# A transformer kernel with routed experts: the last list of a layer in tiles of 128 rows instead of 256, and the experts' weights laid side by side in memory

## The chip, the cores and the metric

The kernel runs on one core of one Trainium2 chip. Its engines work side by side: TensorE (PE in the profile; its weight loads are PEld), VectorE (DVE), ScalarE (ACT), GpSimd (POOL) and SyncE (SP). SP computes nothing here; it reads numbers from memory and issues transfers (DMAs), in the order of its queue. All engines run their own instructions in order and wait for each other by semaphores. The metric is the time of one execution on the device in microseconds (us). A profile is one execution of it, taken by the hardware profiler.

## The reference

All data are float32. The input x has 16 sequences of 256 positions with 128 channels, which is 4096 tokens. Four steps follow each other, each added to x:

```
x = x + attention_a(layernorm(x))    # 16 heads of 8, blocks of 64 positions
x = x + ffn(layernorm(x))            # routed experts, layer 0 of the kernel
x = x + attention_b(layernorm(x))    # 16 heads of 8, over the 16 sequences at one position
x = x + ffn(layernorm(x))            # routed experts again, layer 1 of the kernel
```

The experts' step takes two of eight experts for each token:

```
logits = flat_x @ Wr                           # 4096 x 8
top_vals, top_idx = top_k(logits, 2)
rw = softmax(top_vals)                         # weights of the two experts
g = flat_x @ Wg[e];  u = flat_x @ Wu[e]        # 128 -> 512, for each expert e
h = silu(g) * u
eo = (h @ Wd[e]) / sqrt(12)                    # 512 -> 128
out = sum over the two experts of rw * eo
```

The reference computes all eight experts for each token and uses two; the kernel computes only the two, which is 8192 rows of work in each layer.

## The kernel before

**Tokens and rows.** The tokens are worked on in four quarters (q = 0 to 3) of 1024 tokens each. `router` (L590) normalizes the tokens of a quarter, chooses two experts for each and writes two rows for each token into `sorted_in` in HBM (L699): 128 channels, the weight and the place where the result belongs. Each expert has its own region there, and its rows stand in it in the order in which the quarters arrive. These writes are 16 indirect transfers a quarter, issued by POOL.

**Tiles and lists.** The experts are computed in tiles of TT = 256 rows of one expert. Which expert and which rows a tile has is known only at run time, so it is read from a table. There are three lists of tiles in a layer: the first is made when two quarters are routed (9 tiles), the second after the third (8 tiles), and the last after the fourth (22 tiles), 39 in all. The first two lists hold only full tiles. The last holds all that is left, and since each expert's rest need not fill its tile, it has room for up to seven tiles more than the rows would need. A tile that would reach past its expert's rows is moved back, and rows that were done already, or that are none, are written to places that nobody reads (`behind`). `tile_tables` (L715) computes a list on DVE.

**One tile.** `experts` (L857) runs the tiles of a layer one after another. `fetch` reads the table's row and expert into registers of SP and issues four transfers: the rows `xin` (L866), and from the three weight inputs the expert's `Wg` (L883), `Wu` (L884) and `Wd` (L885) into one tile `w`. It is called two tiles ahead; the buffers of `xin` and `w` are three each. `turned` (L891) transposes `xin` on PE (`xt`, L895), and ACT copies the result to SBUF (`xT`, L897). The hidden size of 512 is cut into four pieces of 128. A tile has two units, each with two of the four pieces: PE computes `g` and `u` for these (L953), each matmul with 256 columns, ACT the tanh (L958), DVE the rest of silu (L959) and the product `h` (L961). One unit later `down` (L900) adds `Wd` times `h` into `acc` (L903), and after a tile's second unit ACT copies `acc` to `yT` (L911), PE transposes it (`y`, L914), ACT scales it into `yo` (L919), and POOL writes the rows to `results` by their places (L926), one indirect transfer for each 128 rows. PSUM holds three buffers for `g` and `u`, one for `acc`.

**Adding the results.** `combine` (L975) reads the two results of each token back (`back`, L979), as soon as enough tiles are done that the quarter's rows must be among them (READY), and adds them to x on DVE (L989). In layer 1 it writes the output (L992). Its transfers stand in SP's queue between those of `fetch`.

**Order.** The order in which the parts are recorded is written out by hand (L1003 to the end): the generators `attention_a`, `attention_b`, `router` and `experts` are advanced step by step, and `weave` lets some run beside others. `units(layer, upto)` advances the experts to a unit. From the counts above it follows for each layer: units 1 to 30 run beside other parts, units 31 to 52 alone behind the last router (BEGIN[0] = 52); in layer 0, units 53 to 60 run beside the first normalization of attention b (FIRST = 60), and the rest to 79 beside that attention by written goals (GOAL = 62, 64, 66, 70, 74, 79); in layer 1 the rest runs alone, with `combine` between, from unit 52 to 66 and to 79. A scheduler then orders the recorded instructions on each engine, and the program is fixed before it runs.

## Time and profile before

| What | us |
|---|---|
| median of 14 runs | 976.18 |
| lowest and highest of them | 971.29, 985.98 |
| the profiled execution | 977.54 |
| its span, first to last instruction | 975.8 |
| PE busy, DVE busy in the span | 860.1, 619.3 |
| ACT busy, POOL busy | 402.8, 359.8 |

The mean granted clock of PE in the profiled execution is 0.938 of full speed. A line of a group or of the timeline names the engine, the kernel's line (L903), the operation, the tile written and the tiles read (`acc<-h,w`), and how many instructions it stands for. One fp32 matmul of the program is two matmul records. The ends of matmuls are modelled, and they are pipelined, so that the starts of two groups, one after the other, tell more than the length of one. In square brackets stands how long the engine was idle before, and what released it. In 107.69 MB and 104922 packets the DMA engines moved 110 GB/s on average.

### The profile page before, as it was taken

To read this page: it belongs to the slowest core of one execution; us is meant where nothing else is said; L and a number is where in the kernel's file an instruction comes from. 1 tells how busy PE (TensorE), PEld (TensorE's weight loads), DVE (VectorE), ACT (ScalarE), POOL (GpSimd) and SP (SyncE) were. 2 spreads that over 40 slices of the span, in tenths; PEclk is the share of its full clock that TensorE was granted. 3 is DMA by queue.
4 is the path that set the end of the run, shared out by engine and by line. 5 is a ranking of instruction groups with operands and counts; after the bars stand their busy time and mean duration, and the time that the engine had idled before them with its cause. 6 is when DMAs were issued, how large, how long until landed. Compare 5 with 4: busy or idle time off the path is not lost.

```text
span 975.8 us, 17640 instructions
## 1 busy us (share of the span) xinstructions
PE 860.1 (88%) x5992; PEld 709.7 (73%) x5992; DVE 619.3 (63%) x1749; ACT 402.8 (41%) x821; POOL 359.8 (37%) x404
## 2 busy tenths in 40 slices
PE   5987888889899999989987859957999999998893
PEld 3666666668788888877866748845777887886782
DVE  4568547657857775467867648835687784556542
ACT  3444334343434444436553435422554433343331
POOL 2112622442363474333121542251407465333322
PEclk9999879789999999999998969978999999999997
DMA  7100100041142476674120402124404466678762
GB/s 187 31 1 1 38 9 1 23 137 45 52 119 93 148 225 193 189 244 130 45 88 1 113 19 88 53 80 130 131 2 124 140 204 187 183 208 266 221 185 81
DMA packets 104922, 107.69 MB, mean 110 GB/s; under 512 B 10688, under 2 KB 80320, under 8 KB 104832
## 3 DMA queue, kind: packets, MB, share of 16 engines
q1 hardware_dynamic: 95024, 87.36, 31.0%
q0 software_dynamic: 9088, 18.89, 5.5%
q8 instruction: 48, 0.79, 0.4%
q10 hardware_dynamic: 720, 0.30, 0.1%
q14 instruction: 42, 0.34, 0.1%
HBM read 83.38 MB, written 23.13 MB: 109 GB/s over the span
## 4 chain that ended last, share of the span: by engine, by line
PE 70%; DVE 10%; DMA 8%; ACT 4%; issue 3%; POOL 3%; SPq 1%; ACTq 0%; POOLq 0%; DVEq 0%
PE g L953 12%; PE u L953 12%; PE acc L903 11%; PE o_A L446 6%; PE sc_A L416 5%; PE t_A L435 3%; DMA back<-results 2%; PE o_B L559 2%; PE v_B L359 2%; PE sc_B L522 2%; DMA results<-yo,to 2%; DMA xin<-sorted_in 2%; PE v_A L359 2%; POOL sorted_in L699 2%; ACT q_A L333 2%
## 5 line engine op out<-in xcount | busy, mean ns | idle before, releaser
L926 POOL DMA_INDIRECT results<-yo,to x156 | 153.9, 986 | 261.5 <-ACT yo L919 229.7
L903 PE MATMUL acc<-h,w 128*128 128x256 f32 x624 | 168.5, 389 | 5.9 <-DVE h L961 5.8
L953 PE MATMUL g<-xT,w 128*128 128x256 f32 x624 | 167.8, 388 | 0.7 <-ACT xT L897 0.5
L953 PE MATMUL u<-xT,w 128*128 128x256 f32 x624 | 165.3, 384 | 3.2 <-DVE th L959 3.2
L699 POOL DMA_INDIRECT sorted_in<-rows,pos_i_F x128 | 125.2, 978 | 89.0 <-DVE pos_i_F L692 34.5
L958 ACT ACTIVATE th<-g 128x512 f32<-128x512 f32 x156 | 93.4, 598 | 148.0 <-PE g L953 147.1
L959 DVE SCALAR_TENSOR_TENSOR th<-th,g 128x512 f32<-128x512 f32 x156 | 106.3, 682 | 74.6 <-ACT th L958 73.0
L903 PEld LDWEIGHTS acc<-h,w 128*128 128x128 f32 x624 | 117.9, 194 | 26.0 <-DVE h L961 9.3
L953 PEld LDWEIGHTS g<-xT,w 128*128 128x128 f32 x624 | 117.7, 195 | 18.1 <-issue 1.8
L953 PEld LDWEIGHTS u<-xT,w 128*128 128x128 f32 x624 | 112.4, 192 | 17.8 <-DVE th L959 4.7
L961 DVE TENSOR_TENSOR h<-th,u 128x512 f32<-128x512 f32 x156 | 106.6, 683 | 13.6 <-PE u L953 3.4
L416 PE MATMUL sc_A<-k_A,q_A 128*128 128x256 f32 x256 | 80.4, 424 | 20.6 <-DVE ex_A L425 13.3
L446 PEld LDWEIGHTS o_A<-va,eT_A 128*64 128x64 f32 x1024 | 62.3, 143 | 16.6 <-issue 7.9
L446 PE MATMUL o_A<-va,eT_A 128*64 128x18 f32 x1024 | 67.0, 216 | 1.4 <-ACT q_A L333 0.8
L416 PEld LDWEIGHTS sc_A<-k_A,q_A 128*128 128x128 f32 x256 | 45.9, 207 | 30.6 <-DVE ex_A L425 12.5
L424 DVE TENSOR_REDUCE mx_A<-sc_A 128x8 f32<-128x512 f32 x64 | 43.3, 682 | 36.7 <-PE sc_A L416 36.3
L911 ACT COPY yT<-acc 128x256 f32<-128x256 f32 x78 | 29.1, 372 | 87.9 <-PE acc L903 87.6
L919 ACT ACTIVATE yo<-y,xin 128x128 f32<-128x128 f32 x156 | 48.5, 366 | 30.7 <-PE y L914 30.6
L429 ACT ACTIVATE ex_A<-ex_A 128x512 f32<-128x512 f32 x64 | 40.1, 634 | 47.2 <-DVE ex_A L425 46.9
L439 ACT COPY eT_A<-t_A 128x512 f32<-128x512 f32 x64 | 36.2, 587 | 55.3 <-PE t_A L435 55.2
L454 POOL TENSOR_TENSOR xq<-xq,att_A 128x128 f32<-128x128 f32 x32 | 14.7, 458 | 116.1 <-DVE att_A L378 103.4
L359 PE MATMUL v_B<-wi_sb,xt_B 128*128 128x128 f32 x256 | 36.0, 292 | 24.1 <-DVE att_B L378 23.2
(173 smaller groups left out, 1294.5 us busy)
## 6 DMA issues: line engine op xcount, KB each, us to landing
w<-in_wg SPq DMA_DIRECT2D x78, 256.0 KB, 2.9
w<-in_wu SPq DMA_DIRECT2D x78, 256.0 KB
w<-in_wd SPq DMA_DIRECT2D x78, 256.0 KB, 4.0
xin<-sorted_in SPq DMA_DIRECT2D x78, 132.0 KB
back<-results SPq DMA_DIRECT2D x16, 512.0 KB, 5.7
results<-yo,to POOLq DMA_INDIRECT x156, 3.5
sorted_in<-zero SPq DMA_DIRECT2D x2, 1056.0 KB
sorted_in<-rows,pos_i_F POOLq DMA_INDIRECT x128, 2.4
```

The lines of the kernel that those rows point to most:

```text
L359: nc.tensor.matmul(pv[:, a * P : (a + 1) * P], lhsT=src[:, g * n + a].rearrange("p r k -> p (r k)"), rhs=w, start=True, stop=True,)
L416: nc.tensor.matmul(sc[:, v * 4 * BS : (v + 1) * 4 * BS], lhsT=qT[:, blk, 2 * v : 2 * v + 2, :].rearrange("p r k -> p (r k)"), rhs=kx[:, :, ...
L424: nc.vector.tensor_reduce(mx[:, 0:8], sc3, AX.X, ALU.max)
L446: nc.tensor.matmul(po[b * BS : (b + 1) * BS, i * 18 : (i + 1) * 18], lhsT=eT[:, b, 2 * v + i % 2, u * BS : (u + 1) * BS], rhs=vt[:, b, 2 * ...
L699: put_row = nc.gpsimd.indirect_dma_start(out=sorted_in[layer], out_offset=bass.IndirectOffsetOnAxis(ap=pos_i[:, k, g : g + 1], axis=0), in ...
L903: nc.tensor.matmul(acc[:, 0:TT], lhsT=w[:, 2, hc * P : (hc + 1) * P], rhs=h[:, j * TT : (j + 1) * TT], start=(hc == 0), stop=(hc == NHC - 1),)
L919: nc.scalar.activation(y[:, b, :], py[:, b * P : (b + 1) * P], AF.Identity, scale=t[:, b, C : C + 1],)
L926: put_row = nc.gpsimd.indirect_dma_start(out=results[layer], out_offset=bass.IndirectOffsetOnAxis(ap=to[:, b : b + 1], axis=0), in_=y[:, b ...
L953: nc.tensor.matmul(p[:, j * TT : (j + 1) * TT], lhsT=w[:, k, hs], rhs=xT, start=True, stop=True,)
L958: nc.scalar.activation(th, pg, AF.Tanh, scale=0.5)
L959: nc.vector.scalar_tensor_tensor(th, th, 1.0, pg, ALU.add, ALU.mult)
L961: beat[0] = nc.vector.tensor_tensor(h, th, pu, ALU.mult).ins
```

## The change

The last list of each layer is made of tiles of TS = 128 rows; the first two lists keep tiles of 256. The bound on the tiles in the last list goes from 22 of 256 rows to 37 of 128, as the room lost at the end of each expert's rows is at most 127 rows instead of 255. A small tile has one unit in place of two: its unit has all four pieces of the hidden size, so that `g`, `u`, the tanh and `h` keep their 512 columns, made of four matmuls of 128 columns in place of two of 256. The units of a layer go from 78 to 71. `fetch` is called up to three tiles ahead in the last list (AHEAD = 3), with five buffers for `xin` and `w`.

All eight experts' `Wg`, `Wu` and `Wd` are copied once, at the start, from the inputs into `w_all` in HBM, where each expert's three parts stand side by side in 128 rows of 1536 numbers. `fetch` then issues one transfer for the weights of a tile. One buffer of `rows` serves the router in place of two. The counts that the order goes by follow: READY counts tiles of 128 rows, BEGIN is now 52, 52, 59, 72, and GOAL 59, 59, 59, 63, 67, 72; FIRST stays 60.

```diff
+TS = P
...
+UNITS = (TOP * NTOK + (NE - 1) * TS) // TS
 LISTS = [full(LISTED)] + [full(n) - full(n - 1) for n in range(LISTED + 1, NQ)]
-LISTS.append(ALL - sum(LISTS))
+LISTS.append(UNITS - sum(LISTS) * (TT // TS))
+SIZES = [TT] * (len(LISTS) - 1) + [TS]
 KMAX = max(LISTS)
+LARGE = sum(LISTS[:-1]) * (TT // TS)
...
-READY = [sum(LISTS[:-1]) + NE - 1] * LISTED
-READY += [(TOP * n * TQ + NE * (TT - 1)) // TT for n in range(LISTED + 1, NQ + 1)]
-NJ = NTOK // TT
+READY = [LARGE + (NE - 1) * (TT // TS)] * LISTED
+READY += [(TOP * n * TQ + NE * (TS - 1)) // TS for n in range(LISTED + 1, NQ + 1)]
+AHEAD = 3
+NJ = NTOK // TS
...
+    p_in = ctx.enter_context(tc.tile_pool(name="p_in", bufs=2 + AHEAD))
...
-    rows = [const.tile([P, NG, TOP, RW], F32, name=f"rows{i}") for i in range(2)]
-    for t in rows:
-        nc.gpsimd.memset(t[:, :, :, C + 1 : RW], 0.0)
+    row = const.tile([P, NG, TOP, RW], F32, name="rows")
+    nc.gpsimd.memset(row[:, :, :, C + 1 : RW], 0.0)
...
+    w_all = dram.tile([NE, P, 3 * HID], F32, name="w_all")
...
+    for i, src in enumerate((wg, wu)):
+        late.append(
+            nc.sync.dma_start(out=w_all[:, :, i * HID : (i + 1) * HID], in_=src)
+        )
+    for n in range(NHC):
+        late.append(
+            nc.sync.dma_start(
+                out=w_all[:, :, 2 * HID + n * C : 2 * HID + (n + 1) * C],
+                in_=wd[:, n * P : (n + 1) * P, :],
+            )
+        )
...
     def experts(layer):
         def fetch(li, i):
             n = f"{layer}_{li}_{i}"
-            t = p3.tile([P, 2, RW], F32, tag="xin", name=f"xin_{n}")
+            size = SIZES[li]
+            t = p_in.tile([P, TT // P, RW], F32, tag="xin", name=f"xin_{n}")
...
             got = nc.sync.dma_start(
-                out=t.rearrange("p b r -> p (b r)"),
-                in_=sorted_in[layer][bass.ds(row, TT)].rearrange("(p b) r -> p (b r)", b=2),
+                out=t[:, 0 : size // P].rearrange("p b r -> p (b r)"),
+                in_=sorted_in[layer][bass.ds(row, size)].rearrange("(p b) r -> p (b r)", p=P),
             )
...
-            w = p3.tile([P, 3, HID], F32, tag="w", name=f"w_{n}")
-            nc.sync.dma_start(out=w[:, 0], in_=wg[bass.ds(e, 1)].rearrange("e c h -> (e c) h"))
-            nc.sync.dma_start(out=w[:, 1], in_=wu[bass.ds(e, 1)].rearrange("e c h -> (e c) h"))
+            w = p_in.tile([P, 3, HID], F32, tag="w", name=f"w_{n}")
             nc.sync.dma_start(
-                out=w[:, 2].rearrange("p (n c) -> p n c", c=C),
-                in_=wd[bass.ds(e, 1)].rearrange("e (n p) c -> p (e n) c", p=P),
-            )
+                out=w.rearrange("p i h -> p (i h)"),
+                in_=w_all[bass.ds(e, 1)].rearrange("e p h -> (e p) h"),
+            )
...
-            nc.scalar.copy(xT, pt[:, 0:TT])
+            nc.scalar.copy(xT[:, 0:size], pt[:, 0:size])
...
-        def down(li, i, t, w, elsewhere, acc, pair, h):
-            for j in range(2):
-                hc = 2 * pair + j
+        def down(li, i, t, w, elsewhere, acc, hcs, h):
+            size = SIZES[li]
+            for j, hc in enumerate(hcs):
                 nc.tensor.matmul(
-                    acc[:, 0:TT], lhsT=w[:, 2, hc * P : (hc + 1) * P],
-                    rhs=h[:, j * TT : (j + 1) * TT],
+                    acc[:, 0:size], lhsT=w[:, 2, hc * P : (hc + 1) * P],
+                    rhs=h[:, j * size : (j + 1) * size],
                     start=(hc == 0), stop=(hc == NHC - 1),
                 )
-            if pair == 1:
+            if hcs[-1] == NHC - 1:
...
-                for b in range(2):
+                for b in bs:
                     put_row = nc.gpsimd.indirect_dma_start(
...
         for at, (li, i) in enumerate(todo):
+            size = SIZES[li]
+            n = CH // size
...
-            for pair in range(2):
+            for part in range(NHC // n):
+                hcs = range(n * part, n * part + n)
...
                 for k, p in ((0, pg), (1, pu)):
-                    for j in range(2):
-                        hs = slice((2 * pair + j) * P, (2 * pair + j + 1) * P)
+                    for j, hc in enumerate(hcs):
                         nc.tensor.matmul(
-                            p[:, j * TT : (j + 1) * TT], lhsT=w[:, k, hs], rhs=xT,
+                            p[:, j * size : (j + 1) * size],
+                            lhsT=w[:, k, hc * P : (hc + 1) * P], rhs=xT[:, 0:size],
                             start=True, stop=True,
                         )
...
-                if pair == 0 and at + 2 < len(todo):
-                    fetched.append(fetch(*todo[at + 2]))
-                if pair == 0 and at + 1 < len(todo):
+                wanted = at + 2 if size == TT else min(begun + 1, at + AHEAD)
+                while begun < len(todo) and part == 0 and begun <= wanted:
+                    fetched.append(fetch(*todo[begun]))
+                    begun += 1
+                if part == 0 and at + 1 < len(todo):
                     xT_next = turned(*todo[at + 1], fetched[0][0])
...
-        known = puts[layer][: 2 * READY[q]]
+        known = puts[layer][: READY[q]]
...
-    EARLY = 2 * sum(LISTS[:-1]) - 4
+    EARLY = LARGE - 4
...
-    UNITS = 2 * ALL + 1
+    STEPPED = UNITS + 1
 
-    BEGIN = [min(2 * n + 1 + LEAD, UNITS) for n in READY]
+    BEGIN = [min(n + 1 + LEAD, STEPPED) for n in READY]
```

In `tile_tables` the sizes 256 become the list's own size; for the last list the tables have 37 columns for 22, and counts in steps of 128 rows, of which there are 32 in place of 16.

## The prediction, made before the changed kernel was run

> **What bounds the kernel now.** I read the busy shares, then stages of the span, then the order of time inside one stage, last the one place where the experts' chain runs bare.
>
> ```profile
> PE 860.1 (88%) x5992; PEld 709.7 (73%) x5992; DVE 619.3 (63%) x1749; ACT 402.8 (41%) x821; POOL 359.8 (37%) x404
> ```
>
> TensorE (PE) leads, but over the whole span. The stages (columns: stretch, its length, busy us of PE, PEld, DVE, ACT, POOL with counts, granted clock, DMA share, GB/s):
>
> ```profile
> 324.00:431.00 107.00, 104.31 (x531) 91.43 (x530) 64.78 (x158) 43.49 (x112) 52.52 (x55) 1.00 0.67 199
> 456.00:518.00 62.00, 59.26 (x577) 49.33 (x576) 47.78 (x110) 34.74 (x59) 9.48 (x9) 0.97 0.23 69
> 518.00:598.00 80.00, 60.54 (x557) 50.04 (x557) 49.06 (x151) 33.13 (x59) 29.55 (x30) 0.83 0.18 54
> 598.00:681.00 83.00, 64.80 (x592) 53.26 (x592) 51.19 (x172) 29.02 (x59) 29.29 (x31) 0.92 0.29 90
> 681.00:762.00 81.00, 76.30 (x655) 62.56 (x655) 61.49 (x192) 40.49 (x77) 35.17 (x35) 0.98 0.30 89
> 825.00:958.00 133.00, 126.94 (x613) 108.56 (x611) 70.29 (x121) 52.03 (x131) 41.81 (x43) 0.99 0.67 200
> ```
>
> Two stretches are the experts' tiles alone: 324 to 431 (end of layer 0's list, before its attention) and 825 to 958 (the whole last list of layer 1, 44 units of half a tile, counted back from the last tanh). There PE is busy 95 to 97% and bounds. In the second attention PE is busy 261 of 306 us: waits decide too. Order of time inside the first kind (start, length, engine, line):
>
> ```profile
> 801.53 0.38 PE L914 MATMUL y<-k_sb,yT 128*128 128x128 f32 x2
> 801.75 0.38 PE L895 MATMUL xt<-k_sb,xin 128*128 128x128 f32 x2
> 801.96 1.03 PE L953 MATMUL u<-xT,w 128*128 128x256 f32 x4
> 802.83 1.03 PE L903 MATMUL acc<-h,w 128*128 128x256 f32 x4
> ...
> 807.15 0.38 PE L914 MATMUL y<-k_sb,yT 128*128 128x128 f32 x2
> ```
>
> One tile is 807.15 - 801.53 = 5.62 us, a unit 2.81 us. Four 256-column records go out in 802.83 - 801.96 = 0.87 us (0.217 each); the last one's result is there 0.16 us after the next may start. Each matmul of the program is two such records. A `g` (0.87 us) stands between `acc` and `y`: the copy `yT` hides under it.
>
> For 128 columns the attention shows the rate: eight records in 599.49 - 598.60 = 0.89 us, 0.111 each.
>
> ```profile
> 598.60 1.05 PE L359 MATMUL v_B<-wi_sb,xt_B 128*128 128x128 f32 x8
> 599.49 0.39 PE L522 MATMUL sc_B<-k_B,q_B 128*128 128x128 f32 x2
> ```
>
> The last tile of the run has nothing beside it, so each hop of its chain is bare:
>
> ```profile
> 957.37 0.69 DVE L961 TENSOR_TENSOR h<-th,u 128x512 f32<-128x512 f32 x1
> 958.11 1.13 PE L903 MATMUL acc<-h,w 128*128 128x256 f32 x4 [0.26 <-DVE h L961]
> 959.34 0.37 ACT L911 COPY yT<-acc 128x256 f32<-128x256 f32 x1 [2.27 <-PE acc L903]
> 959.76 0.44 PE L914 MATMUL y<-k_sb,yT 128*128 128x128 f32 x2 [0.52 <-ACT yT L911]
> 960.24 0.63 ACT L919 ACTIVATE yo<-y,xin 128x128 f32<-128x128 f32 x2 [0.53 <-PE y L914]
> ```
>
> A hop from engine to engine costs 0.03 to 0.10 us, and a PE group that has waited takes 0.10 us more (1.13 against 1.03), as its weight load is no longer hidden.
>
> ```profile
> L911 ACT COPY yT<-acc 128x256 f32<-128x256 f32 x78 | 29.1, 372 | 87.9 <-PE acc L903 87.6
> L439 ACT COPY eT_A<-t_A 128x512 f32<-128x512 f32 x64 | 36.2, 587 | 55.3 <-PE t_A L435 55.2
> ```
>
> **Part 1, PE work.** The last list goes from 22 tiles (44 units) to 37 tiles, one unit each. A small unit is 24 records x 0.111 + 2 transposes x 0.108 = 2.88 us of PE, against 2.81. If PE stayed the bound, a layer's last list would go from 22 x 5.62 = 123.6 to 37 x 2.88 = 106.6 us, 17 less. By the Trainium skill's "Perfetto Trace Analysis", Matmuls, larger matmuls are more efficient than smaller ones; the rows above price that at 2.88 to 2.81, 2.5%, so the rule alone would not turn the sign.
>
> **Part 2, the chain of a small unit: a new wait.** In the built program of the changed kernel, PE's instructions in the last list stand in this order: rest of `acc`(k-1), `y`(k-1), `xt`(k+1), first part of `acc`(k), `g`(k+1), `u`(k+1), rest of `acc`(k), `y`(k) and so on, with 1 and 3 of the four `acc` matmuls before `g` in turns. No `g` stands between `acc` and `y` any more, and `xt`(k+1) has only one `acc` part before the `g` that needs it. ACT's order is tanh(k), `yT`(k-1), `yo`(k-1), `xT`(k+1). Everything on PE queues behind the waiting `y`, and `xT` queues behind `yo`. From the moment `u`(k) is issued (0):
> - `h`(k): `g`(k) was issued at -0.89, result -0.73, tanh (0.60) from -0.69 to -0.09, L959 (0.69) to 0.63, L961 (0.69, 0.10 later) 0.73 to 1.42; `acc`(k) may start at 1.47.
> - One `acc`(k-1) left: issued 0.22, result 0.39, `yT` from 0.49. A 128-column copy is not in the trace; from 372 ns at 256 and 587 at 512 I get 265 (ends: 213, ACT's shortest row, and 372): 0.75. `y` 0.80, result 1.13 (0.44 for two, less 0.11), `yo` (0.31, half of 0.63) 1.17 to 1.48, `xT` 1.52 to 1.79, `g` from 1.84. Meanwhile `acc`(k) one matmul 1.47 to 1.79. `g` and `u` 1.78 + 0.10 exposed load: the next unit's zero is 3.72.
> - Three left: all of the `y` to `xT` path is 0.44 later, `g` from 2.28 (`acc`(k), three matmuls, 1.57 to 2.23), next zero 4.16.
>
> Mean 3.94 us a unit, PE busy 2.88 of it. I take 3.94; the ends are 2.88 (all waits filled) and 4.6 (the sum with the copy at 372 ns and two more hops of 0.1 on each side, rounded up).
> - Layer 0, alone: units 35 to 52 are 18 before and after (both lists reach unit 34 with the large tiles and run alone to unit 52): 18 x (3.94 - 2.81) = +20.3.
> - Layer 1, 825 to 958: 133 us = 44 x 2.81 = 123.6 and 9.4 of stalls, mostly `xin` transfers behind combine's loads on SP's queue. After: 37 x 3.94 = 145.8. Stalls: between 0 and 9.4; fetches now run three tiles ahead and two transfers (not four) stand in SP's queue per tile, so transfer waits fall, but combine's twelve DVE additions of 0.6 to 0.7 us among these tiles now fall into a chain that DVE is part of. I take 4: 149.8, +16.8.
> - Layer 0, units 53 to 60 beside the first normalization of the second attention: same count, half hidden by its work; 0 to 8 x 1.13 = 9; I take +3.
>
> **Part 3, seven units fewer beside the second attention.** Units 61 to 79 (19) become 61 to 72 (12), and the written goals now put none beside the attention's first three halves (2 each before). PE work taken away: 7 x 2.88 = 20. In 518 to 598 PE idles 19 of 80 us and the clock is 0.83, so work taken from there shortens little, and where units covered waits the waits become bare. Between -20 and 0 (a loss if the clock falls further); I take -10.
>
> **Part 4, transfers.** Per tile one transfer of 768 KB and one of 66 in place of four. SP issues in 0.33 us each and idles most of the time: 0. PE's waits from 825 to 960 name `xin`, never `w`. The Trainium skill's "Perfetto Trace Analysis", DMA Optimizations, says that batching transfers under 2 KB into 4 to 8 KB can improve throughput dramatically; a weight row here goes from 0.5 and 2 KB to 6 KB. By the rows (DMA busy 0.67, no wait on `w`) the gain is 0; the rule would matter if DMA became the bound. Traffic per small tile: 786 + 68 + 66 KB in 3.94 us = 233 GB/s, over the 200 of the stretch at 0.67; 200 / 0.67 = 298 would be full. Hidden; without that cover (rate 200) a tile takes 4.6 us, +36 over 55 tiles.
> The copy of all weights (six transfers, 6.3 MB each way, behind the loads and fills on SP's queue): at the 191 GB/s of the first 25 us it takes 33 to 66 us, ending before 90; the first fetch issues at about 207, and DMA is nearly idle from 50 to 200. Cost 0, at most 2 for the loads that share its engines. Without that cover 66.
>
> **Part 5, the rest.** The last list's tables: eight DVE operations grow from 506 to 851 elements (0.67 to about 1.06) and two from 384 to 768 (0.55 to about 0.95): +3.9 us per layer. In layer 1 the table is ready at 798.6, while the fetch that reads it issues at 817.9 behind the last rows' scatter on POOL (to 814.8): cover 19 us, cost 0; without it 3.9 a layer. One `rows` buffer for two: the next router comes some 80 us later (`y_B` at 516, 596, 760), scatter long done: 0. One put instead of two at the end (1.27 us) and shorter last pieces: -1.5. Combine's loads before the second attention held an `xin` back by 3.0 us of PE idle near 430; with units of 3.94 the puts waited for are older: -2.
>
> **Sum** against the profiled execution, 977.54 us (span 975.8 and 1.7 around it): 20.3 + 16.8 + 3 - 10 - 1.5 - 2 = +26.6, 1004.1. That execution is 1.4 above the median of the 14 runs (976.18), so 1003 for a median.
>
> **Rivals.**
> 1. PE stays the bound (waits filled, unit 2.88): 18 x 0.07 = +1.3; 106.6 + 4 - 133 = -22.4; -10 - 1.5 - 2: -34.6, 942. This is the faster end. For it: PE is 95% busy in these stages today. Against it: in the new order nothing that is ready can pass the waiting `y`. It decides below the unit time at which the sum is zero: 55 units x p + 4 - 50.6 - 133 + 3 - 10 - 3.5 = 0, p = 3.46 us.
> 2. DMA becomes the bound: 4.6 us a tile if it moves no more than 200 GB/s, 1039. Against it: 24 us slices of the page at 266 GB/s.
> 3. The clock falls. After 1.24 and 0.45 us of PE idle near 820, the next 3.4 us ran at half speed:
>
> ```profile
> 820.00 0.44 PE L895 MATMUL xt<-k_sb,xin 128*128 128x128 f32 x2 [1.24 <-DMA xin<-sorted_in]
> 821.30:824.70 3.40, 3.40 (x10) 2.69 (x9) 1.61 (x3) 0.00 (x0) 0.96 (x1) 0.50 0.84 251
> ```
>
> A small unit idles 1.06 of 3.94 us, about 0.9 in such a window, half of what stood there; so I expect no fall. If every fourth of the 63 windows in 55 x 3.94 us fell, at 1.7 us each: +27, 1030. The Trainium skill's "TensorE: Matmul & The Clock Gate", Part 1, lets the clock fall after a whole idle window of about 3.4 us; the row above fell after half of one. By the rule this rival costs 0, by the row it stays possible.
> 4. Seven units fewer save all their PE work (-20, not -10): 993.
> 5. Not what it says: excluded for the counts (37 tiles of 128 rows stand in the built program).
>
> **How the numbers follow.** Chances: the chain as summed 0.55 (own range 988 to 1020), with case 4 0.14, cases 2 and 3 together 0.13, unit times under the limit of case 1 0.15, near it 0.03. The range leaves out most of case 1 and the far ends of 2 and 3, which is 2 in 10: 972 to 1030. No change means within 0.3%, about what this kernel's runs can tell apart (3 us): faster 0.15, same 0.04, slower 0.81.
>
> **What would show it.** In the stretch of the last lists: `y` rows on PE with idle "<-ACT yT" of 0.3 to 0.6 us each and `g` rows with "<-ACT xT" or `acc` rows with "<-DVE h"; th rows of ACT (one a unit) 3.9 us apart, PE busy about 75%, clock 1.00, DMA share about 0.75. PE's total falls (some 2 x 17 us) while the span grows. Wrong if th rows are under 3.5 us apart, if `xt` idles "<-DMA" every tile (case 2), or if the clock of these stretches is under 0.95 (case 3). Part 3 is wrong if the second attention, from the first `v_B` to the last `y_B` (307 us), does not get 5 to 15 us shorter.

## The result, and the profile after

The changed kernel takes 1033.59 us (median of 10 runs, 1028.35 to 1037.55), the kernel before 976.18; the ratio is 1.059, 95% interval 1.056 to 1.062. The prediction said 1003 and 972 to 1030: the sign is right, the size is half. The profiled execution has a span of 1032.9 us against 975.8, +57.1, at the same granted clock (0.939 and 0.938). One thing about the runs below has to be known: they fell on chips of two speeds, on which the kernel before took 973 to 976 or 1040 to 1050, so each ratio is to the kernel before on the same chip, and the text says "the slower chip" where it was that one.

The first line of the page (busy us of each engine, share of the span, instructions):

```profile
PE 862.3 (83%) x6684; PEld 722.4 (70%) x6684; DVE 607.4 (59%) x1751; ACT 401.6 (39%) x853; POOL 347.7 (34%) x389
```

PE's share falls from 88 to 83%, but its busy time does not fall. The stages that answer to those of the prediction (stretch, length, busy us of PE, PEld, DVE, ACT, POOL with counts, clock, DMA share, GB/s): layer 0's units 35 to 52 alone, the four quarters of the second attention, and the last list of layer 1 from unit 35.

```profile
377.00:450.00 73.00, 60.99 (x469) 54.91 (x470) 28.45 (x58) 25.43 (x74) 18.30 (x19) 0.99 0.76 243
486.00:541.00 55.00, 44.59 (x493) 36.25 (x493) 38.04 (x94) 27.11 (x42) 5.40 (x5) 0.91 0.07 23
541.00:619.00 78.00, 56.88 (x543) 47.15 (x543) 43.39 (x144) 28.81 (x50) 26.29 (x27) 0.80 0.14 41
619.00:692.00 73.00, 64.26 (x663) 57.82 (x663) 47.74 (x155) 29.69 (x66) 27.73 (x29) 0.91 0.42 131
692.00:792.00 100.00, 84.38 (x701) 69.32 (x700) 69.00 (x211) 42.66 (x81) 35.41 (x36) 0.97 0.29 89
858.00:1014.60 156.60, 127.12 (x944) 114.01 (x943) 61.20 (x121) 50.81 (x146) 36.16 (x37) 0.96 0.71 234
```

In the first and the last PE is busy 84 and 81% where it had been 95 to 97: these stretches are bound by something else now. The same 18 units took 50.6 us before, with PE busy throughout. Counted from the start of one tanh to that of another ("units 35 to 52" ends at the tanh of unit 53, "units 53 to 60" at that of unit 60), the difference is made up so:

| Stretch | before | after | difference | predicted |
|---|---|---|---|---|
| start to unit 35 of layer 0 | 374.5 | 376.9 | +2.4 | 0 |
| units 35 to 52 | 50.6 | 72.9 | +22.3 | +20.3 |
| units 53 to 60 | 28.7 | 34.1 | +5.4 | +3 - 2 |
| to the first v_B | 3.0 | 1.7 | -1.3 | 0 |
| second attention | 304.0 | 306.1 | +2.1 | -10 |
| to unit 35 of layer 1 | 64.7 | 66.5 | +1.8 | 0 |
| rest of the last list | 130.5 | 156.4 | +25.9 | +16.8 |
| after the last tanh | 19.8 | 18.3 | -1.5 | -1.5 |
| sum | 975.8 | 1032.9 | +57.1 | +26.6 |

Inside the first stretch, PE, ACT and DVE in order of time (start, length, engine, line; in brackets the idle time before and what ended it):

```profile
400.51 1.06 PE L976 MATMUL u<-xT,w 128*128 128x128 f32 x8
401.34 0.69 DVE L983 SCALAR_TENSOR_TENSOR th<-th,g 128x512 f32<-128x512 f32 x1 [2.14 <-ACT th L982]
401.41 0.83 PE L917 MATMUL acc<-h,w 128*128 128x128 f32 x6
402.33 0.27 ACT L925 COPY yT<-acc 128x128 f32<-128x128 f32 x1 [1.02 <-PE acc L917]
402.65 0.33 PE L929 MATMUL y<-k_sb,yT 128*128 128x128 f32 x1 [0.41 <-ACT yT L925]
402.81 0.16 DVE L939 TENSOR_TENSOR to<-xin,behind 128x1 int32<-128x1 f32 x1 [0.78 <-DMA xin<-sorted_in]
402.81 0.27 PE L909 MATMUL xt<-k_sb,xin 128*128 128x128 f32 x1
402.92 0.69 DVE L985 TENSOR_TENSOR h<-th,u 128x512 f32<-128x512 f32 x1
403.01 0.37 ACT L934 ACTIVATE yo<-y,xin 128x128 f32<-128x128 f32 x1 [0.42 <-PE y L929]
403.28 0.26 ACT L911 COPY xT<-xt 128x128 f32<-128x128 f32 x1
403.66 0.94 PE L917 MATMUL acc<-h,w 128*128 128x128 f32 x6 [0.57 <-DVE h L985]
404.43 1.06 PE L976 MATMUL g<-xT,w 128*128 128x128 f32 x8
```

This is the order that the prediction gave: PE stands 0.41 us before `y`, whose copy `yT` nothing hides, `xt` queues behind it, `xT` behind `yo`. One thing is there that it did not give: `to` (L939) stands on DVE between the two halves of silu and waits 0.78 us for the rows of a later tile; `h` and the `acc` behind it are late by that. The waits of PE in the whole run say the same (us in total, times, longest); before, `y` had hardly waited for `yT` (0.5 us) and `acc` 5.8 us for `h`:

```profile
PE y L929 <- ACT yT L925: 25.0, 60, 0.7
PE acc L917 <- DVE h L985: 22.5, 39, 2.0
PE ot_B L515 <- DVE att_B L393: 9.4, 3, 7.8
```

The last tile, bare as before, and the copies by their shape (busy, mean ns, idle before):

```profile
1016.69 1.16 PE L917 MATMUL acc<-h,w 128*128 128x128 f32 x8 [0.34 <-DVE h L985]
1018.26 0.33 PE L929 MATMUL y<-k_sb,yT 128*128 128x128 f32 x1 [0.41 <-ACT yT L925]
1018.62 0.37 ACT L934 ACTIVATE yo<-y,xin 128x128 f32<-128x128 f32 x1 [0.42 <-PE y L929]
...
L934 ACT ACTIVATE yo<-y,xin 128x128 f32<-128x128 f32 x142 | 48.4, 367 | 44.4 <-PE y L929 43.1 <-DMA results<-yo,to 0.8 <-DMA back<-results 0.4
L925 ACT COPY yT<-acc 128x128 f32<-128x128 f32 x74 | 19.8, 267 | 68.6 <-PE acc L917 68.6
```

The copy takes 267 ns (estimated: 265), `yo` 367 (taken: 310).

### The profile page after: what moved, and what is told of

The parts are those of the page before. It is cut to its first block, busy times and chain, and to the rows that moved or that the text cites. A ratio compares the mean times of both kernels' runs of the same rounds, so it can differ in the third digit from the quotient of the medians.

```text
span 1032.9 us, 18843 instructions
## 1 busy us (share of the span) xinstructions
PE 862.3 (83%) x6684; PEld 722.4 (70%) x6684; DVE 607.4 (59%) x1751; ACT 401.6 (39%) x853; POOL 347.7 (34%) x389
## 5 line engine op out<-in xcount | busy, mean ns | idle before, releaser
L943 POOL DMA_INDIRECT results<-yo,to x142 | 141.1, 994 | 302.0 <-ACT xT L911 148.5
L917 PE MATMUL acc<-h,w 128*128 128x128 f32 (+1 forms) x864 | 169.0, 320 | 22.9 <-DVE h L985 22.5
L983 DVE SCALAR_TENSOR_TENSOR th<-th,g 128x512 f32<-128x512 f32 x142 | 96.8, 682 | 154.3 <-ACT th L982 153.8
L976 PE MATMUL g<-xT,w 128*128 128x128 f32 (+1 forms) x864 | 159.1, 319 | 7.3 <-ACT xT L911 3.9
L976 PE MATMUL u<-xT,w 128*128 128x128 f32 (+1 forms) x864 | 155.3, 316 | 6.1 <-DVE th L983 6.1
L917 PEld LDWEIGHTS acc<-h,w 128*128 128x128 f32 x864 | 130.0, 196 | 42.9 <-DVE h L985 33.5
L976 PEld LDWEIGHTS u<-xT,w 128*128 128x128 f32 x864 | 125.4, 198 | 13.5 <-DVE th L983 8.4
L925 ACT COPY yT<-acc 128x128 f32<-128x128 f32 (+1 forms) x108 | 32.4, 300 | 116.9 <-PE acc L917 116.9
L929 PE MATMUL y<-k_sb,yT 128*128 128x128 f32 x142 | 37.5, 303 | 29.9 <-ACT yT L925 25.0
L929 PEld LDWEIGHTS y<-k_sb,yT 128*128 128x128 f32 x142 | 19.5, 141 | 48.2 <-ACT yT L925 37.8
```

The lines of the kernel that those rows point to most:

```text
L917: nc.tensor.matmul(acc[:, 0:size], lhsT=w[:, 2, hc * P : (hc + 1) * P], rhs=h[:, j * size : (j + 1) * size], start=(hc == 0), stop=(hc == ...
L929: nc.tensor.transpose(py[:, b * P : (b + 1) * P], yT[:, b * P : (b + 1) * P], ident)
L943: put_row = nc.gpsimd.indirect_dma_start(out=results[layer], out_offset=bass.IndirectOffsetOnAxis(ap=to[:, b : b + 1], axis=0), in_=y[:, b ...
L976: nc.tensor.matmul(p[:, j * size : (j + 1) * size], lhsT=w[:, k, hc * P : (hc + 1) * P], rhs=xT[:, 0:size], start=True, stop=True,)
L983: nc.vector.scalar_tensor_tensor(th, th, 1.0, pg, ALU.add, ALU.mult)
```

## Experiments on the chain of a small unit

Theory A: the order on PE and the copies behind it set the unit. Against it stood the hop from `xT` to `g` alone (B), the transfers (C), and a higher price of a 128-column matmul (D).

**xT two tiles ahead** (with three `xT` buffers, and four of `yo` in place of six for room; the rows are also fetched four tiles ahead, into six buffers, and the weights' transfers are queued apart from them):

```diff
-                if part == 0 and at + 1 < len(todo):
-                    xT_next = turned(*todo[at + 1], fetched[0][0])
+                while part == 0 and len(xTs) < (1 if size == TT else 2) and at + len(xTs) + 1 < len(todo):
+                    xTs.append(turned(*todo[at + len(xTs) + 1], fetched[len(xTs)][0]))
```

> The changed kernel, but in the last list the rows are transposed and copied (xt, xT) two tiles ahead in place of one, so that g no longer waits for xT; three xT buffers, the rows fetched four tiles ahead, four buffers for yo in place of six to make room. The instructions of PE stand in the same order as in the changed kernel: rest of acc(k-1), y(k-1), xt, part of acc(k), g(k+1), u(k+1). Theory A (the order on PE: everything queues behind the y that waits for its copy yT): y is issued 0.8 us after u and the acc part behind it waits for h at 1.47, so the unit stays at 3.6 to 4.1 us, 35 units of layer 0 alone and layer 1 no shorter, total 1025 to 1036. Theory B (the hop xT to g sets the unit): without it a unit falls to about 3.3, total about 1000.

One run on the slower chip: 1069.99 against 1049.72, 1.019. The expectation held that the order on PE stays. It did not: in layer 0 the scheduler now put half of the next `g` between `acc` and `y`, and the units there are 3.08 us apart, all but a few; units 35 to 52 take 56.9 us in place of 73. Near the end of layer 1 the old order was left, and there the units are 4.03 us apart, as in the changed kernel, although `xT` is long there:

```profile
442.20 0.61 PE L986 MATMUL g<-xT,w 128*128 128x128 f32 x4
442.77 0.33 PE L935 MATMUL y<-k_sb,yT 128*128 128x128 f32 x1
...
1036.49 0.33 PE L935 MATMUL y<-k_sb,yT 128*128 128x128 f32 x1 [0.41 <-ACT yT L931]
1036.66 0.27 PE L915 MATMUL xt<-k_sb,xin 128*128 128x128 f32 x1
1037.16 0.94 PE L923 MATMUL acc<-h,w 128*128 128x128 f32 x6 [0.23 <-DVE h L995]
1037.93 1.06 PE L986 MATMUL g<-xT,w 128*128 128x128 f32 x8
```

Upper two rows, layer 0: no bracket, `y` does not wait. Lower rows, layer 1: 0.41 before `y`, 0.23 before `acc`. So taking away the hop B alone, in the old order, gains nothing; what counts is a piece of `g` between `acc` and `y`, and the early `xT` is what lets it stand there.

**The order laid down**, on top of `xT` two tiles ahead, and with a quarter of the weights' bytes:

```diff
+                if size == TS and back:
+                    home(*back.pop(0), ends[0])
                 if pending is not None:
-                    down(*pending)
+                    down(*pending, ends[1] if size == TS else None)
```

`home` is the part of `down` from `y` on, recorded one unit later; it puts y(k-1) behind the last matmul of g(k+1), and `down` puts acc(k) behind u(k+1). The quarter, in which a small tile fetches one piece of each weight and uses it four times, so that three quarters of the weights are left out of the computation:

```diff
-                out=w.rearrange("p i h -> p (i h)"),
-                in_=w_all[bass.ds(e, 1)].rearrange("e p h -> (e p) h"),
+                out=w[:, :, 0:P] if size == TS else w,
+                in_=w_all[bass.ds(e, 1)].rearrange("e p (i h) -> (e p) i h", i=3)[
+                    :, :, 0 : P if size == TS else HID
+                ],
```

> As the run with xT two tiles ahead, and the order of PE in the last list is laid down: xt(k+2), g(k+1), u(k+1), y(k-1), acc(k). yT has a g and a u to hide under, h too. Nothing else is changed, the matmuls are the same 24 records and 2 transposes. Theory A (order on PE): the unit falls from 4.05 to PE's own work, 2.88 to 3.1 us; 18 units of layer 0 alone give 18 to 20 us back, units 53 to 60 about 4, the last list of layer 1 some 30 to 40: total 970 to 985. Theory C (the transfers bound: 854 KB a unit at 266 GB/s are 3.2 us): unit 3.2 to 3.5, total 985 to 1000. Theory D (a 128-column matmul costs PE more than its record rate): unit stays over 3.6, total over 1015.

> The changed kernel, but a small tile's weight transfer brings only the first of the four pieces of Wg, Wu and Wd (192 KB in place of 768) and the matmuls use that piece four times, so that part of the computation is left out; numbers of instructions and transfers and the order on PE stay. Theory A (order on PE): in the undisturbed stretches the unit stays at 3.6 and 4.1 us in turns, layer 0 alone gives 0 to 2 us, only stalls of late transfers in the last list of layer 1 go: total 1018 to 1031. Theory C (transfers bound): units of 3.0 to 3.4 us, total under 1000. For the clock: if it rises above 0.95 in the last list of layer 1 although PE idles as much as before, the transfers had a part in its fall.

> As the run with the order of PE laid down, but with only a quarter of each small tile's weights transferred (192 KB a tile, part of the computation left out). It prices the transfers once PE no longer waits in its queue. If PE's own work bounds the run with the order laid down, this one is the same within 5 us, unit 2.88 to 3.0. If the transfers bound it there, this one is shorter by 55 units times the difference, 10 to 30 us.

One run each on the slower chip, against 1049.72: order laid down 1053.08 (1.003), quarter of the weights 1079.53 (1.028), both 1041.23 (0.992). Layer 0 alone, units 35 to 52, in this order:

```profile
407.70:464.30 56.60, 53.73 (x467) 52.18 (x466) 25.74 (x53) 25.27 (x73) 16.68 (x18) 1.00 0.80 265
```
```profile
401.70:474.40 72.70, 60.09 (x469) 53.77 (x468) 29.37 (x60) 25.41 (x73) 18.63 (x20) 1.00 0.37 106
```
```profile
407.80:460.80 53.00, 52.53 (x468) 52.14 (x467) 26.05 (x53) 25.33 (x73) 16.77 (x18) 1.00 0.40 114
```

With the order laid down the 73 us become 56.6, with steps of 2.90 us between longer ones of up to 4.5. That is no less than `xT` two tiles ahead has by itself there (56.9); in the last list of layer 1 it is, 135.4 us for 142.9. A quarter of the bytes alone changes nothing: 72.7 us at 106 GB/s, steps of 3.63 and 4.08 as before; C is out for the changed kernel. Both together give 2.90 in every step but the first two: this is PE's own work (predicted 2.88), D is out. The 3.6 us between the first and the third are what the transfers cost once the chain is out of the way.

## Experiments on the queues of DVE and SP

**`to` behind its own h.** The line on DVE in the changed kernel with the longest wait, in the fourth quarter of the second attention:

```profile
781.71 0.16 DVE L939 TENSOR_TENSOR to<-xin,no_pads 128x2 int32<-128x2 f32 x1 [10.06 <-DMA xin<-sorted_in]
```

```diff
+                tc.add_manual_dep(at_place.ins, h[1].name, NOSYNC, reason="order on DVE")
```

> The changed kernel, but the small DVE operation `to` of a tile, which needs the tile's rows (xin), stands on DVE behind that tile's own h; in the changed kernel it stands wherever the scheduler put it, up to two units earlier, and DVE waits there for a transfer (53.9 us in all, 10.06 at 781 in the fourth quarter of the second attention, 3.52 at 983). The order on PE stays. Theory T (these waits hold up h, and in the attention the work behind them): the second attention gets 6 to 10 us shorter than 306, the last list of layer 1 some 4 to 8: ratio to the kernel before 1.043 to 1.050, against 1.059. Rival U (what DVE waits for, PE waits for as well, a few places on): ratio 1.056 to 1.062.

> The changed kernel with `to` behind its own h on DVE, again. Where the changed kernel has 306 us from first v_B to last y_B and 152 to 156 in the last list of layer 1, theory T (DVE waits for xin at `to`, 10.06 us in the fourth quarter and 6.36 in the third): 295 to 300 and 146 to 150, ratio 1.040 to 1.048. Rival U (PE waits for the same transfer anyway): 304 to 308 and 151 to 156, ratio 1.055 to 1.060.

> The changed kernel with `to` behind its own h on DVE, beside the unchanged one. Theory T: 6 to 12 us less in the second attention and the last list of layer 1 together, the ratio lower by 0.006 to 0.012. Rival U (PE waits for the same transfers): within 0.004 of it.

> The changed kernel unchanged, on the chip of the other runs, where the kernel before took 1040 in place of 976: it gives their comparisons a base. If `to` and out_x have each cost 8 to 14 us (theories T and S), the ratio to the kernel before is 1.053 to 1.062, as where the change was measured (1.059). If moving them gained nothing, it is 1.043 to 1.049, what those two runs had here.

> The changed kernel unchanged, as the base of the run beside it. On the slower chip (before at 1040): the same 57 us more would be a ratio of 1.055; if the slower chip's own waits cover part of the small tiles' chain, 1.045 to 1.05.

On the slower chip it had 1.045 (1.037 to 1.053) and 1.046 (1.040 to 1.052), where the changed kernel was never run. The third time both ran on the faster chip: the changed kernel 1.060 (1.055 to 1.064), with `to` moved 1.038 (1.034 to 1.041), 1032.97 and 1011.91 us. That is 21 us for an operation of 0.16 us, more than theory T said; U is out. The changed kernel by itself had 1.058 (1.050 to 1.066) once more. The third and fourth quarter of the attention, the changed kernel first, then with `to` moved:

```profile
614.90:688.20 73.30, 64.52 (x662) 57.76 (x660) 47.80 (x156) 29.87 (x66) 27.44 (x29) 0.91 0.40 130
688.20:790.00 101.80, 86.96 (x699) 71.41 (x700) 68.80 (x210) 42.67 (x81) 35.75 (x37) 0.93 0.29 88
```
```profile
613.80:679.10 65.30, 60.47 (x662) 54.32 (x660) 47.42 (x155) 29.90 (x66) 27.34 (x29) 0.97 0.40 131
679.10:773.30 94.20, 84.74 (x699) 69.26 (x700) 68.33 (x210) 42.62 (x82) 33.62 (x35) 0.98 0.28 92
```

The same instructions take 8.0 and 7.6 us less; the two first quarters are the same within 0.4. The attention goes from 305.3 to 289.3, by 16.0, where DVE had waited 6.19 us at `to` in the third quarter and 10.12 in the fourth. The attention's own work stood on DVE behind these waits, `vb` in the third quarter and `att_B` in the fourth: PE's waits for them were 4.2 and 8.7 us and are 0.5 and 0.8 with `to` moved. The clock rises too, 0.91 to 0.97 and 0.93 to 0.98; how much of the 16.0 us is the wait itself and how much the lower clock that came with it was not separated. Both waits are at tiles of 256 rows (`no_pads`, 128x2) of layer 1's first lists, not at small tiles. The last list gives 3.7, layer 0 alone 2.1.

**out_x behind later fetches.** The queue of SP in the changed kernel, in the last list of layer 1:

```profile
931.41 0.36 SPq L898 DMA_DIRECT2D w<-w_all  x1
935.71 6.48 SPq L1019 DMA_DIRECT2D out_x<-xq  x4
942.25 0.60 SPq L1006 DMA_DIRECT2D back<-results  x1
943.43 0.34 SPq L881 DMA_DIRECT2D xin<-sorted_in  x1
```

From 932 to 943 nothing is fetched: `out_x` waits for the additions on DVE, and the fetches stand behind it. A step of 7.91 us from 944.7 follows, in which `g` waits for `w` until 950.57.

```diff
+                tc.add_manual_dep(put.ins, fetch_last[0].name, NOSYNC, reason="order on SP")
...
+        adds = [combine(1, part) for part in range(2 * q, 2 * q + 2)]
+        for add in adds:
+            next(add)
+        outs.append((BEGIN[q] + 3, adds))
```

> The changed kernel, but the transfers of the output (out_x) of a quarter are recorded three units later and stand on SP behind the fetches of those units, where the changed kernel has fetches queued behind an out_x that waits for the additions on DVE (24.2 us in all, longest 9.8). Theory S (SP's queue: the fetches come late, and these are the units of 5 to 8 us in the last list of layer 1): that list, 156 us from unit 35 to the last tanh, gets 8 to 14 us shorter, ratio 1.045 to 1.051. Rival V (the combine's additions on DVE and the traffic of its transfers make the long units): less than 4 us, ratio 1.055 to 1.062.

Slower chip: 1.046 (1.038 to 1.054). The last list from unit 35 is 147.7 us; the run with other goals, on the same chip and with this list unchanged, has 152.8, and the changed kernel's three profiles 151.6 to 156.4. So it is 4 to 9, between what S and V said: SP's queue is a part of the long units, not all of it. The clock goes with these lengths, 0.99 in the list of 147.7 us and 0.98, 0.97 and 0.96 in those of 151.6, 154.3 and 156.4, so a part of the 4 to 9 us may be the clock.

**Goals.**

```diff
-    GOAL = [FIRST + (BEGIN[2] - FIRST) * (k + 1) // 3 for k in range(3)]
-    GOAL += [BEGIN[2] + (STEPPED - BEGIN[2]) * (k + 1) // 3 for k in range(3)]
+    GOAL = [FIRST + (STEPPED - FIRST) * (k + 1) // 6 for k in range(6)]
```

> The changed kernel, but the written goals spread the last 12 units of layer 0 evenly over the six halves of the second attention (62, 64, 66, 68, 70, 72 in place of 59, 59, 59, 63, 67, 72). Theory G (units cover waits of the attention; where none stand the waits are bare, and where four or five stand PE is the bound): from first v_B to last y_B 306 us becomes 296 to 301, ratio 1.048 to 1.055. Rival H (the attention's own chain and the clock set its time, wherever the units stand): 304 to 308, ratio 1.056 to 1.062.

Slower chip: 1.040 (1.033 to 1.048). The attention is 322.4 us against 327.5 in the run with `out_x` moved, whose attention is that of the changed kernel: 5 less, the third quarter 12 shorter and the second 4.5 longer. This does not show G: on the slower chip the engines also idle with no releaser on the core (last section), and in the attention these gaps add up over the engines to 50 us here and 74 in the other run, a difference larger than the 5 us. The ratios of the three runs (`to`, `out_x`, goals) overlap and don't rank them.

## Experiments on the whole, and on one part alone

**All three repairs** (xT ahead and the order, `to`, `out_x`), then with the even goals as well:

> All three repairs of the chain and the queues together: xT two tiles ahead and the order of PE laid down (units of 2.90 us in the earlier look), `to` behind its own h, out_x behind the later fetches; goals as in the changed kernel. If the lost time is these three and they add up: 18 units of layer 0 alone -18, units 53 to 60 -4, the last list of layer 1 from 156 to 112 or 118, the second attention -6 to -10: 955 to 970 on the scale where before is 976, ratio 0.978 to 0.994. If transfers bound instead once the order is right: ratio 0.995 to 1.01.

> The changed kernel with all three repairs (xT two ahead and the order on PE laid down, `to` behind its h, out_x behind later fetches), again. By the stages: layer 0 alone 73 to 54 us, units 53 to 60 34 to 32, the second attention 306 to 296, the last list of layer 1 154 to 125 or less: 1032 - 19 - 2 - 10 - 29 = 972, ratio 0.99 to 1.005. If the three are the whole loss and the 37 tiles ran at PE's 2.90 us, that list would take 108: ratio 0.975 to 0.985; what lies between is then the transfers and the combine.

> As the run with all three repairs, and the goals spread evenly over the six halves of the second attention (62 to 72). Theory G (units cover waits of the attention): the second attention another 3 to 8 us shorter than with the goals of the change, ratio 0.983 to 0.998. Rival H (the attention's own chain): within 2 us of it.

All on the slower chip: 1.004 (1.000 to 1.009) and 1.001 (0.996 to 1.006); with even goals 0.994 (0.990 to 0.998). Layer 0 alone is 53.5 to 55.4 us, the last list 124.1 to 124.9, where the kernel before has 50.6 and 130.5. The first ratio lies in the range that its expectation gave to the transfers, but what is missing lies in the attention: 324.6 and 325.7 us, where 296 was expected. On the slower chip there was nothing at `to` to take away: in the runs there that leave `to` in its place (`out_x`, goals, quarter of the weights), DVE waits at `to` in the attention for at most 0.5 us, where the faster chip has 6.2 and 10.1. The even goals take the attention to 316.9, with the same reservation as above (gaps of 57 us for 79). So in the experts' lists the loss of the change is the chain of the small unit and the places of a few instructions in two queues; repaired, 37 small tiles are as good as 22 large ones, hardly better. The three repairs together were never run on the faster chip. The list stays 20 us above 36 steps of 2.90: with the order laid down and a quarter of the bytes it was 117.5 us, still with one step of 11.35, in which `xt` waits 5.47 us for rows whose fetch stood behind `back` and `out_x`.

**One part of the change alone:** large tiles with `w_all`, and small tiles without it.

```diff
-            nc.sync.dma_start(out=w[:, 0], in_=wg[bass.ds(e, 1)].rearrange("e c h -> (e c) h"))
-            nc.sync.dma_start(out=w[:, 1], in_=wu[bass.ds(e, 1)].rearrange("e c h -> (e c) h"))
...
+                out=w.rearrange("p i h -> p (i h)"),
+                in_=w_all[bass.ds(e, 1)].rearrange("e p h -> (e p) h"),
```

> One part of the change alone: the kernel before with tiles of 256 rows in all lists, but the weights copied side by side at the start and fetched by one transfer a tile. The prediction put this part at 0 (the copy of 6.3 MB each way lies where the DMA engines idle, no instruction waits on w): ratio 0.996 to 1.004. Rival: the copy holds up the loads of the start, 1.004 to 1.01. Other rival: fewer packets and a shorter SP queue bring xin earlier, of whose waits the kernel before has 9 us in the last list of layer 1: 0.990 to 0.996.

> The other part alone: tiles of 128 rows in the last list, but no copy of the weights; each tile fetches Wg, Wu and Wd in three transfers from the inputs, in packets of 2 KB and 512 B, as the kernel before does. If the transfers had cover to spare (854 KB in 4 us are 214 GB/s, the stretch before had 200 at a share of 0.67), the ratio is that of the changed kernel within 0.005. If the single transfer carries the small tiles, units rise over 4.1 us in layer 0 alone and the ratio is 1.07 to 1.10.

Faster chip, side by side: large tiles with `w_all` 1.007 (1.004 to 1.011), small ones without it 1.067 (1.057 to 1.076), the changed kernel 1.058 (1.050 to 1.066). So `w_all` costs the large tiles some 7 us by the ratio. In the profiles they lie in the last list, 137.4 us for 130.5, where one step became 11.2 us: PE waited 4.5 us for rows whose fetch stood behind `back` on SP and landed 6.6 us after its issue, and the 3.4 us after it ran at a clock of 0.50. The other rise, 4 us before unit 35, is within what runs differ there (374.5 to 379.6 without the copy, 376.9 to 380.8 with it). For the small tiles one transfer in place of three is worth some 8 us (1040.6 against 1032.3; these runs don't overlap, the intervals of the ratios do), and not in the undisturbed units: layer 0 alone is 73.4 us with three transfers, as with one (71.6 to 73.4). Its expectation had the same ratio within 0.005 or 1.07 to 1.10; it is neither.

**The two queue repairs in the kernel before**, nothing of the change:

> The kernel before, tiles of 256 rows, with the two repairs of the queues and nothing of the change: `to` behind its own h on DVE, out_x behind two later fetches on SP. DVE waits 66.0 us for xin at `to` in the kernel before, 11.66 of it at 653 in the second attention, and the last list of layer 1 has 9.4 us of stalls. If these waits hold up others there too: ratio 0.98 to 0.993, and it beats both kernels. If PE hides them, as it is busy 95% in these lists: 0.996 to 1.003.

> The kernel before with the two repairs of the queues, again, beside the small tiles with theirs: 0.982 to 0.992 as before. If small tiles pay once their chain and the queues are repaired, the run with all three repairs is below this one; if not, the tiles of 256 rows stay the better.

0.987 (0.978 to 0.995) on the faster chip, 964.41 us, and 0.993 (0.989 to 0.997) on the slower, beside 0.994 of the small tiles with all repairs. It beats both kernels with large tiles; on the faster chip the second attention goes from 304.0 to 294.6 and the last list from 130.5 to 125.7 (130.2 on the slower). The small tiles with all three repairs (1.001 beside it) are not below it; they come level only with the even goals.

## Why the prediction was right and wrong

- **Part 1, a small unit of 2.88 us of PE:** shown, 2.90 where nothing else bounds. That PE's total would fall by 2 x 17 us is wrong: it is 862.3 for 860.1. In layer 0 alone, 18 units count as 61.0 us busy, 3.39 each, and as 53.7 with the order laid down: the busy time of the same instructions depends on the waits between them (a group of eight is 1.16 us behind a wait and 1.06 otherwise). Busy time was no measure of the work taken away.
- **Part 2, the chain:** shown by the order laid down. The undisturbed steps are 3.63 and 4.07 us, predicted 3.72 and 4.16, `y` waits 0.41 each time. Layer 0 alone gave +22.3 for +20.3; `to` is 2.1 of it.
- **Part 2, "Stalls: between 0 and 9.4 ... I take 4":** a step that failed. The last list is 36 steps from unit 35; at the mean 3.85 they are 138.6 us, and the three profiles have 151.6 to 156.4: 13 to 18 of stalls. The runs show what is in them: `to` 3.7, SP's queue 4 to 9; a quarter of the bytes gave 146.4 on the slower chip, 6 less than the unchanged list there. These overlap, and the clock is in them too (0.99 in the lists of the last two), so how the 13 to 18 divide stays open. The prediction took 4 because fetches would run further ahead; it did not count the fetches that stand behind `out_x`, nor `to`.
- **Part 3, -10 in the second attention:** the other step that failed, and the larger miss. Without the waits at `to`, the large tiles have 294.6 us and the small ones 289.3 (one profile each): 7 units fewer are worth -5.3, inside -20 to 0. But moving `to` gains 9.4 us before and 16.0 after; these +6.6, which the prediction put at nothing, turn the -5.3 into the +1.3 of the two profiles (305.3 and 304.0). By the marks used here the attention is 304.0 us before, not the 307 of the prediction's last paragraph. The prediction never looked at what `to` waited for; the trace of before had it 39 times, 66.0 us in all, 11.7 the longest.
- **The -2 near 430, and +3 for units 53 to 60:** +5.4 in place of +1. The steps there go up to 6.8 us. `to` waits 1.35 us in the step just before (5.51 us, 3.77 where `to` was moved), and the first step of the stretch is 5.12 for 4.38; the rest was not taken apart.
- **Part 4, transfers at 0:** right in that no transfer set the unit, wrong for its size: one transfer is worth some 8 us to small tiles and costs large ones 7. The prediction weighed the Trainium skill's "Perfetto Trace Analysis", DMA Optimizations, by which batching small transfers can improve throughput. In these runs it is worth 0.8% to the small tiles, nothing of it in layer 0 alone, and with large tiles a late fetch on SP outweighed it.
- **Part 5:** the end is 1.5 us shorter, as said; tables and the copy of the weights cannot be told from the scatter of the stretches they lie in (+1.8 and +2.4).
- **Rivals:** PE bound (942) was reached in single steps only with the order laid down; DMA bound was ruled out for the changed kernel by the quarter of the bytes. The clock fell a little in the last list (0.96) and not in layer 0 alone (0.99), where PE idles 12 of 73 us in pieces of up to 0.6 us and one of 1.59. In the last list it fell in the step of 7.91 us: PE was busy 1.33 of the 3.4 us up to 950.6, with no idle piece over 1.66, and the next 3.4 us ran at a granted 0.55 (the eight records of `g` took 2.04 us there). By the Trainium skill's "TensorE: Matmul & The Clock Gate", Part 1, a whole idle window lowers the clock. Here, as in the prediction's row at 820, less than a whole window was enough. An estimate from the mean clock of that list: 4% of 156.6 us, so at most 6 us.

What the range left out made the kernel slower: above all instructions that wait for a transfer in an in-order queue and hold up what stands behind them. The range ended 3.6 us below the result.

## What to carry to other kernels

When a tile is halved, write down the order of one unit on every engine, and ask what stands between a matmul and the copy that follows it: here a `g` that was lost there cost 0.7 to 1.2 us a tile (steps of 3.63 and 4.07 us for 2.90), and putting it back took 73 us to 57. Look in the trace for the smallest instruction that waits for a transfer in an in-order queue, also where it seems to cost nothing: moving a 0.16 us operation behind its own tile's `h` gave 21 us in the changed kernel, and with `out_x` moved too 9 in the kernel before (4 on the slower chip). A queue that issues both the loads ahead and the stores behind should have the stores recorded late.

## What was not expected of the hardware

The same program runs 64 to 78 us longer on the slower chip, and mostly not in the experts' lists: layer 0 alone is 71.6 to 73.4 us for the changed units on both. In all traces from there, ACT and DVE (and at times PE) idle before an instruction for up to 11.7 us with no releaser on the core ("remote"); the traces of the faster chip have this nowhere. None of these gaps lies in layer 0 alone or in the last list of layer 1 behind unit 35. The longest in sum, in the kernel before with two repairs on the slower chip (us in total, times, longest):

```profile
ACT th L961 <- remote: 33.8, 6, 11.1
DVE rec_B L378 <- remote: 22.8, 3, 10.4
DVE rec_A L378 <- remote: 18.8, 3, 9.7
```

What these wait for, the runs don't show. They have a bearing on what moving `to` gains: it had 1.045 on the slower chip and 1.038 on the faster. With `to` in its place the attention on the slower chip is 327.5 us, with `to` moved 324.9 (same chip), so that most of the 16.0 us of the faster chip are not to be had there, as the waits at `to` are not there either. That the transfers catch up while the engines stand in the other gaps is likely, but not shown.
